# A planner's table of costs and ranks: chained list scatters, gating durations from the trace, a later rank for early gating

## The chip, the core and the metric

The kernel runs on one core of one Trainium2 chip. Five engines work side by side, each through its own instructions in the order in which they were emitted: PE (TensorE, matmuls and transposes into PSUM), DVE (VectorE), ACT (ScalarE), POOL (GpSimd) and SP (SyncE, which here only issues DMAs). They meet through semaphores. The metric is the device time of one execution in microseconds. Times inside a profile are counted from the start of its span.

## What is computed

One transformer block with adaptive layer norm, on x of shape 2 x 2048 x 256 in float32: causal attention with two query heads over one shared key and value head, and then a mixture of eight experts, in which each token uses those experts whose gate lies above a threshold of its own.

```python
sa, ca, ga, sb, cb, gb = six rows of silu(c) @ wmod           # per batch
h = layernorm(x) * (1 + ca) + sa
x = x + ga * attention(h)                                     # causal, rope, 2 heads, D = 256
h = layernorm(x) * (1 + cb) + sb                              # the "hx" of the kernel
gate = softmax(h @ Wg + bg);  thr = sigmoid(h @ Wt + bt) * 0.125
w = max(gate - thr, 0);  w = w / sum(w)                       # 8 experts
x = x + gb * sum_e w_e * (gelu(h @ W1_e + b1_e) @ W2_e + b2_e)
```

## The kernel before

**Two stages.** The 4096 tokens are 32 tiles of 128. In the attention stage every tile is normalised, projected, attended over all earlier tiles of its batch, projected back and normalised again; its rows go to a table in HBM (`feats`), its gate logits to `lg`. Then the experts stage runs hardware loops over lists of tokens: for each expert, items of 256 tokens are gathered from `feats`, turned by a DMA transpose, sent through both weight matrices and added to the output by scatter.

**Groups of tiles.** The tiles come in groups: (0, 4), (1, 4) three times, then two groups of two tiles and four of one, where the first number is the batch and the second the tiles. `q` is the number of tiles before the group, so it is 0, 4, 8, 12, 16 and 20 for the six groups of four. A tile's steps have the rank of its number (`tile_steps`, argument `r`).

**A tile's steps that matter here.** `moments` (L407 to L422) takes mean and variance on DVE (`stats`) and then 1/std on POOL (`rstd`, two small operations, L418 and L419; called `rstda` before attention and `rstdf` after it). `hx` (L667 and L670) is the second normalised row, on DVE; its second operation needs `rstdf`. `halves` (L677, POOL) splits it for the table, `turn_h` (L692, PE) transposes it to `ph`, `logits` (L701, PE) makes the gate logits. Within attention, `score` (L528) makes scores, `keep` (L539, DVE) copies them out and takes their maxima, `top` (L546) joins these to `nmx`, `exp` (L555, ACT) exponentiates, `turn_p` (L601, PE) transposes the probabilities to `ptr`, `pT_out` (L605, ACT) copies them out and `pav` (L611, PE) multiplies by the values.

**Gating of a group** (`gate_steps`, from L716) is six steps: `below` (DVE), `exps` (ACT), `weigh` (DVE; each group's waits for the one before, through `order_w`), `count` (PE, one PSUM bank of the six of the kind "ps", returned by `places`), `spread` (DVE) and `places` (DVE), which writes the place of every token in every expert's list. Then one `scatter` per tile (L807, an indirect DMA that POOL issues) writes the first expert's list, `lists[0]`, in HBM. The lists of the other experts are written later, inside the experts' loops.

**The planner.** No step is emitted at once. `plan.add(engine, cost, do, after, take, give, rank, late)` records it: cost is how long the step holds its engine, `after` names the steps it needs, `take` and `give` count buffers, `late` is time after the cost until its results can be used. `Plan.run` (L59) then plays an imagined clock: whenever an engine is free, the ready step with the lowest rank starts; a result can be used by the next engine 0.12 us later (`LINK`). The order in which steps start there becomes the order of instructions on each engine. Nothing else of the plan reaches the chip: there, engines wait for semaphores, which the framework places by the tiles and tensors that instructions share. Two scatters into `lists[0]` write the same tensor, and so the later one waits on the chip until the earlier one has landed, whether the plan says so or not.

**The end of the stage.** Once the first 24 tiles have been gated, the first 512 entries of the first list are fixed; they are read back (`read_front`, L903) after their scatters, and two items of expert 0 are worked through on PE while the last tiles finish (rank 1000, that is, whenever nothing else is ready). After the last scatter the whole first list is read (L1002), and the next item's rows are gathered, turned and copied to `xT`. Then the experts stage begins.

Of the kernel before, what the change touches and what calls it, by code (L numbers as in the profile page):

```python
# [192 lines left out]
def attention(  # L193
# [16 lines left out]
    def ps_tile(name):  # L210
        return psum.tile([P, 512], F32, tag="ps", name=name)
# [88 lines left out]
    def load_expert(e):  # L300
# [13 lines left out]
        after=[s_sc], rank=first,  # L314
# [24 lines left out]
    for b in range(B):  # L339
# [43 lines left out]
        r = 0.6 + 2 * b  # L383
# [6 lines left out]
    for e in range(RES):  # L390
# [3 lines left out]
                rank=8.0 + 4 * e,  # L394
# [29 lines left out]
    def tile_steps(b, i, r, group, g):  # L424
# [4 lines left out]
        n = (i + 1) * P  # L429
        nch = -(-n // SC)  # L430

        def add(eng, cost, do, after=(), **how):
            return plan.add(eng, cost, do, after=after, rank=r, **how)
# [129 lines left out]
        for h in range(NH):  # L563
            kept = []
            for c in range(nch):
# [4 lines left out]
                    give=["qT"] if (h, c) == (NH - 1, nch - 1) else [],  # L570
# [7 lines left out]
        n_e = {}  # L578
# [16 lines left out]
        def turn_p(c0, m):  # L595
            st["ptr"] = ps_tile(f"ptr{u}_{c0}")
            ptr = st["ptr", c0] = st["ptr"].rearrange("p (c h t) -> p c h t", c=2, h=NH)
            for j in range(m):
                for h in range(NH):
                    s = st["s", h, (c0 + j) * P // SC]  # L600
                    nc.tensor.transpose(ptr[:, j, h, :], s[:, ds((c0 + j) * P % SC, P)], ident)  # L601

        def pT_out(c0, m):
            pT = st["pT", c0] = work([P, 2, NH, P], "pT", f"{u}_{c0}")
            nc.scalar.copy(pT[:, :m], st["ptr", c0][:, :m])  # L605

        def pav(c0, m):
            if c0 == 0:
                st["pav"] = psum_v.tile([P, 512], F32, tag="pav", name=f"pav{u}")
            for j in range(m):  # L610
                nc.tensor.matmul(  # L611
                    st["pav"][:, : NH * P], v[:, c0 + j, :],
                    st["pT", c0][:, j].rearrange("p h t -> p (h t)"),
                    start=(c0 + j == 0), stop=(c0 + j == i),
                )

        n_p = []
        for c0 in range(0, i + 1, 2):
            m = min(2, i + 1 - c0)
            c = c0 * P // SC  # L620
            done = c0 + m == i + 1 or (c0 + m) * P % SC == 0
            n_t = add(
                "PE", 0.155 * 2 * m, lambda c0=c0, m=m: turn_p(c0, m), [n_e[0, c], n_e[1, c]],
                take=["ps"] + (["pav"] if c0 == 0 else []), give=["s", "s"] if done else [],
            )
            n_o = add(
                "ACT", 0.2 + 0.26 * m, lambda c0=c0, m=m: pT_out(c0, m), [n_t], take=["pT"],
                give=["ps"],
            )
            n_p.append(  # L630
                add(
                    "PE", 0.435 * m, lambda c0=c0, m=m: pav(c0, m),
                    [n_o] + n_p[-1:] + [ready_v[b, c0 + j] for j in range(m)], give=["pT"],
                )
            )
# [80 lines left out]
    def gate_steps(b, i0, m, q, group, after):  # L716

        u = f"_{b}_{i0}"
        at = b * NT + i0
        r = q + m - 1.0  # L720
        st = group

        def add(eng, cost, do, after=(), **how):
            return plan.add(eng, cost, do, after=after, rank=r, **how)
# [81 lines left out]
        def scatter(j):  # L806
            nc.gpsimd.indirect_dma_start(  # L807
                out=lists[0],
                out_offset=bass.IndirectOffsetOnAxis(ap=place[:, at + j, 0:1], axis=0),
                in_=entry[:, at + j, 0, :],  # L810
                in_offset=None,
            )

        n = add("DVE", 0.35, below, after)
        n = add("ACT", 0.5, exps, [n])
        n = add("DVE", 1.6, weigh, [n] + order_w)
        order_w[:] = [n]
        n_c = add("PE", 0.3, count, [n], take=["ps"])
        n_w = add("DVE", 1.2, spread, [n])
        n = add("DVE", 1.0, places, [n_c, n_w], give=["ps"])  # L820
        for j in range(m):
            listed.append(plan.add(
                "POOL", 1.27, lambda j=j: scatter(j), after=[n], rank=r + 10.0, late=3.0
            ))
        return n

    order_w, listed, last_exp = [], [], []
    groups = [(0, 4), (1, 4)] * 3 + [(0, 2), (1, 2), (0, 1), (1, 1), (0, 1), (1, 1)]
    begun, q = [0] * B, 0
    for b, m in groups:  # L830
        group, ends = {}, []
        for j in range(m):
            ends.append(tile_steps(b, begun[b] + j, float(q + j), group, j))
        last = gate_steps(b, begun[b], m, q, group, ends)
        begun[b] += m
        q += m
        if q == AHEAD_TILES:
            listed_ahead = list(listed)

            def filled(group=group):  # L840
                pf = ps_tile("pf")
                nc.tensor.matmul(pf[:, :1], ones, group["sum"][:, :1], start=True, stop=True)
                nc.vector.tensor_scalar(flag, pf[:, :1], float(AHEAD * TI), None, ALU.is_ge)

            n_flag = plan.add("PE", 0.2, filled, after=[last], take=["ps"], give=["ps"], rank=q)
# [25 lines left out]
    def low(eng, cost, do, after=(), **how):  # L871
        return plan.add(eng, cost, do, after=after, rank=1000.0, **how)
# [44 lines left out]
    n_w = low("DVE", 0.5, weights_ahead, [n_front, n_flag])  # L917
    before_gelu = list(last_exp)
    for k in range(AHEAD):
# [23 lines left out]
        def first(f0, st=st, k=k):  # L943
            st["ph", f0] = ph = ps_tile(f"pha_{k}_{f0}")
            for f in (f0, f0 + 1):
                for j in range(KD):
                    nc.tensor.matmul(
                        ph[:, ts(f - f0, TI)], weights[0][0][:, j, ts(f, P)], st["xT"][:, j, :],
                        start=(j == 0), stop=(j == KD - 1),
                    )  # L950
# [9 lines left out]
        def second(c, f0, st=st, k=k):  # L960
            if (c, f0) == (0, 0):
                st["py"] = ps_tile(f"pya_{k}")
            for f in range(f0, f0 + NF // 2):
                nc.tensor.matmul(
                    st["py"][:, ts(c, D)], st["g", f // 2 * 2][:, ds(f % 2 * TI + c * P, P)], weights[0][1][:, f, :],
                    start=(f == 0), stop=(f == NF - 1),
                )
# [13 lines left out]
        for f0 in range(0, NF, 2):  # L981
            n = low(
                "PE", 1.74, lambda f0=f0, first=first: first(f0), [n_x, l_first[0]] + before_gelu,
                take=["ps"], give=["s"] if f0 == NF - 2 else [],
            )
# [4 lines left out]
        n = None  # L990
        for c in range(CI):
            for f0 in (0, NF // 2):
                n = low(
                    "PE", 1.74, lambda c=c, f0=f0, second=second: second(c, f0),
                    n_a + ([n] if n is not None else []),
                    take=["ps"] if (c, f0) == (0, 0) else [],
                    give=["s"] * (NF // 2) if (c, f0) == (CI - 1, NF // 2) else [],
                )
# [17 lines left out]
    n = low("DVE", 0.4, behind, [n_s, n_flag])  # L1016
# [405 lines left out]
```

## Time and profile before

| what | us |
|---|---|
| median of three runs | 1696.54 (1695.61 to 1699.3) |
| the profiled execution | 1694.8 |
| its span, first to last instruction | 1693.0 |
| first matmul of the experts' loops | 526.1 |
| last matmul of the attention stage ends at about | 518.8 |
| first and last scatter into the first list start at | 79.9, 504.1 |

The profiled execution is 1.8 us above its span, and 1.7 us below the median of the runs. Everything that the planner orders lies in the first 526 us; the other 1167 us belong to loops whose order is written out by hand. Lines of the timeline have: start, duration, engine, line, operation, output and inputs, count, and in brackets how long the engine stood idle before, and for what.

### The profile page before, as it was taken

Reading aid. Unit: us, or ns where it says so; the run is one execution under the profiler, and the core shown is the slowest. Engines: PE = TensorE matmul, PEld = TensorE weight load, DVE = VectorE, ACT = ScalarE, POOL = GpSimd, SP = SyncE. Lnnn points to the kernel's source line nnn. Section 1 sums busy time; section 2 is a strip of 40 time slices with the busy share of each in tenths; the row PEclk is TensorE's granted clock in tenths of the full one; section 3 lists DMA queues with packets and bytes.
Section 4 is the critical chain, followed back from the end, with each engine's and each line's share of the span. In section 5 each row is a group of like instructions: output and inputs, shape, how many; then the busy total and the mean of one; then the engine's idle time right before and its main releaser. Section 6 shows DMA issues by size and latency. Waiting matters only on the chain.

```text
span 1693.0 us, 26695 instructions
## 1 busy us (share of the span) xinstructions
PE 1627.9 (96%) x7666; PEld 1354.3 (80%) x7666; DVE 677.9 (40%) x2220; ACT 575.1 (34%) x1390; POOL 855.9 (51%) x991
## 2 busy tenths in 40 slices
PE   6898999999998997999999999999999999999997
PEld 3666666677777886888888888888888888888886
DVE  5886666566652322223332222223222232222322
ACT  1544555555551222222222222222322232222222
POOL 2332322111125777765776775676677467744443
PEclk9999999999999998999999999999999999999998
DMA  6310100000013335333434533433533343333333
GB/s 210 102 36 26 38 20 29 22 11 19 14 40 92 59 62 109 56 63 62 103 61 64 109 59 66 106 61 59 106 59 59 65 63 57 64 56 59 65 56 47
DMA packets 166046, 106.36 MB, mean 63 GB/s; under 512 B 111137, under 2 KB 157345, under 8 KB 165857
## 3 DMA queue, kind: packets, MB, share of 16 engines
q0 software_dynamic: 42064, 46.84, 17.3%
q1 hardware_dynamic: 116048, 46.22, 11.8%
q10 hardware_dynamic: 7872, 12.58, 2.3%
q8 instruction: 26, 0.43, 0.1%
q14 instruction: 36, 0.29, 0.1%
HBM read 50.39 MB, written 31.87 MB: 49 GB/s over the span
## 4 chain that ended last, share of the span: by engine, by line
PE 60%; DMA 3%; POOL 2%; issue 2%; POOLq 0%; DVE 0%; SPq 0%; DVEq 0%
PE h L1142 30%; PE y L1133 30%; DMA xp<-xr 2%; POOL out L1285 1%; DMA xr<-feats,at 1%; POOL list L1275 0%; DMA out<-yo,who 0%; POOL xr L1254 0%; POOLq L1035 0%; POOL out L1317 0%; POOL at L1296 0%; POOLq L1083 0%; POOLq L1296 0%; DVE yo L1232 0%; DVE xT L896 0%
## 5 line engine op out<-in xcount | busy, mean ns | idle before, releaser
L1142 PE MATMUL h<-xT,w 128*128 128x256 f32 (+1 forms) x2752 | 659.8, 373 | 16.3 <-DVE xT L1196 9.0
L1133 PE MATMUL y<-w,g 128*128 128x256 f32 x2640 | 654.2, 379 | 0.0
L1168 ACT ACTIVATE g<-h,b_sb 128x256 f32<-128x256 f32 (+1 forms) x688 | 319.6, 465 | 847.5 <-PE h L1142 844.8
L1142 PEld LDWEIGHTS h<-xT,w 128*128 128x128 f32 x2752 | 515.6, 192 | 85.4 <-DVE xT L1196 10.5
L1133 PEld LDWEIGHTS y<-w,g 128*128 128x128 f32 x2640 | 499.2, 190 | 65.2
L1285 POOL DMA_INDIRECT out<-yo,who x173 | 283.0, 1636 | 212.8 <-DVE yo L1232 160.6
L1196 DVE COPY xT<-xp 128x512 uint16<-128x512 uint16 x172 | 68.4, 439 | 613.9 <-PE h L1142 581.2
L1275 POOL DMA_INDIRECT list<-new,to x228 | 235.4, 1032 | 99.3 <-POOL new L1270 46.7
L1254 POOL DMA_INDIRECT xr<-feats,at x172 | 173.7, 1010 | 100.9 <-POOL at L1296 70.2
L611 PE MATMUL pav<-pT,v 128*128 128x256 f32 x544 | 144.8, 389 | 0.5 <-ACT pT L605 0.5
L528 PE MATMUL psc<-kT,qT 128*128 128x512 f32 (+3 forms) x320 | 144.2, 536 | 0.6 <-ACT qT L517 0.2
L539 DVE TENSOR_SCALAR_CACHE_REDUCE s<-psc 128x512 f32<-128x512 f32 (+3 forms) x160 | 95.8, 605 | 78.1 <-PE psc L528 59.2
L555 ACT ACTIVATE s<-s,nmx 128x512 f32<-128x512 f32 (+3 forms) x160 | 103.8, 651 | 53.7 <-DVE nmx L546 53.4
L611 PEld LDWEIGHTS pav<-pT,v 128*128 128x128 f32 x544 | 95.9, 192 | 26.3 <-issue 16.4
L1220 DVE TENSOR_TENSOR yb<-y,b_bc 128x256 f32<-128x256 f32 x165 | 62.7, 420 | 132.4 <-PE y L1133 132.4
L605 ACT COPY pT<-ptr 128x512 f32<-128x512 f32 (+1 forms) x144 | 76.8, 563 | 50.9 <-PE ptr L601 28.9
L418 POOL TENSOR_SCALAR rstdf<-mvf 128x1 f32<-128x1 f32 x32 | 8.7, 270 | 166.7 <-DVE mvf L414 70.5
L807 POOL DMA_INDIRECT list<-entry,place x32 | 33.8, 1056 | 101.3 <-DVE place L804 75.1
L601 PEld LDWEIGHTS ptr<-ident,s 128*128 128x128 f32 x544 | 65.4, 143 | 21.3 <-ACT s L555 8.7
L601 PE MATMUL ptr<-ident,s 128*128 128x128 f32 x544 | 76.6, 277 | 4.5 <-ACT s L555 4.4
L1211 DVE SCALAR_TENSOR_TENSOR gate<-gb_bc,mcur,part 128x256 f32<-128x256 f32 x172 | 75.8, 482 | 3.0
L528 PEld LDWEIGHTS psc<-kT,qT 128*128 128x128 f32 x320 | 56.9, 191 | 15.3 <-issue 6.2
(157 smaller groups left out, 1076.1 us busy)
## 6 DMA issues: line engine op xcount, KB each, us to landing
w<-in_w ACTq DMA_DIRECT2D x12, 1024.0 KB, 8.0
x<-in_x SPq DMA_DIRECT2D x32, 128.0 KB, 2.1
out<-x SPq DMA_DIRECT2D x32, 128.0 KB, 1.7
w<-in_w SPq DMA_DIRECT2D x4, 1024.0 KB, 9.1
feats<-hp SPq DMA_DIRECT2D x32, 128.0 KB, 1.7
list<-new,to POOLq DMA_INDIRECT x228
out<-yo,who POOLq DMA_INDIRECT x173, 3.9
xr<-feats,at POOLq DMA_INDIRECT x172, 2.8
```

The lines of the kernel that those rows point to most:

```text
L528: nc.tensor.matmul(ps[:, :w], st["qT"][:, h, :], kT[:, ds(c * SC, w)], start=True, stop=not last)
L539: nc.vector.tensor_scalar(s[:, :w], st["sc", h, c][:, :w], 1.0, None, ALU.mult, ALU.max, accum_out=st["mx", h][:, c : c + 1],)
L555: nc.scalar.activation(s[:, :w], s[:, :w], AF.Exp, bias=st["nmx", h], accum_out=st["den"][:, h, c : c + 1],)
L601: nc.tensor.transpose(ptr[:, j, h, :], s[:, ds((c0 + j) * P % SC, P)], ident)
L605: nc.scalar.copy(pT[:, :m], st["ptr", c0][:, :m])
L611: nc.tensor.matmul(st["pav"][:, : NH * P], v[:, c0 + j, :], st["pT", c0][:, j].rearrange("p h t -> p (h t)"), start=(c0 + j == 0), stop=(c ...
L1133: last = pe.matmul(ys[c], gs[f % 4][:, ts(c, P)], weights[e][1][:, f, :], start=(f == 0), stop=(f == NF - 1),)
L1142: last = pe.matmul(hs[f % 4][:, :w], weights[e][0][:, k, ts(f, P)], xT[:, k, :w], start=(k == 0), stop=(k == KD - 1),)
L1168: act.activation(gs[f % 4][:, :w], hs[f % 4][:, :w], AF.Gelu_apprx_tanh, bias=b1_sb[:, at : at + 1],).then_inc(sem["act"], 1)
L1254: pool.indirect_dma_start(out=xr[:, ts(c, 2 * D)], out_offset=None, in_=feats, in_offset=bass.IndirectOffsetOnAxis(ap=at[:, c : c + 1], ax ...
L1275: pool.indirect_dma_start(out=lists[e], out_offset=bass.IndirectOffsetOnAxis(ap=to[:, j : j + 1], axis=0), in_=new[:, j, :], in_offset=Non ...
L1285: pool.indirect_dma_start(out=rows, out_offset=bass.IndirectOffsetOnAxis(ap=who[:, c : c + 1], axis=0), in_=yo[:, c, :], in_offset=None, b ...
```

## The change

Three kinds of edit, all in numbers that the planner reads; no instruction's work is altered.

- Scatters into the first list: each now names the scatter before it as one that it needs; the cost goes from 1.27 to 1.1 and the lateness from 3.0 to 1.5.
- Durations: `below` 0.35 to 0.4, `weigh` 1.6 to 1.4 + 0.2 per tile of the group (2.2 for four tiles, 1.8 for two, 1.6 for one), `spread` 1.2 to 1.4, `places` 1.0 to 1.2; a transpose in `turn_p` 0.155 to 0.12.
- Rank of gating: for groups of four tiles it is raised by 8 - 2 * (q // 8): by 8 for q = 0 and 4, by 6 for 8 and 12, by 4 for 16 and 20. Ranks of gating are then 11, 15, 17, 21, 23 and 27 where they were 3, 7, 11, 15, 19 and 23. The scatters' rank stays 10 above it.

```diff
-                "PE", 0.155 * 2 * m, lambda c0=c0, m=m: turn_p(c0, m), [n_e[0, c], n_e[1, c]],
+                "PE", 0.12 * 2 * m, lambda c0=c0, m=m: turn_p(c0, m), [n_e[0, c], n_e[1, c]],
...
-        r = q + m - 1.0
+
+        r = q + m - 1.0 + (8.0 - 2.0 * (q // 8) if m == 4 else 0.0)
...
-        n = add("DVE", 0.35, below, after)
+        n = add("DVE", 0.4, below, after)
         n = add("ACT", 0.5, exps, [n])
-        n = add("DVE", 1.6, weigh, [n] + order_w)
+        n = add("DVE", 1.4 + 0.2 * m, weigh, [n] + order_w)
         order_w[:] = [n]
         n_c = add("PE", 0.3, count, [n], take=["ps"])
-        n_w = add("DVE", 1.2, spread, [n])
-        n = add("DVE", 1.0, places, [n_c, n_w], give=["ps"])
+        n_w = add("DVE", 1.4, spread, [n])
+        n = add("DVE", 1.2, places, [n_c, n_w], give=["ps"])
+
         for j in range(m):
             listed.append(plan.add(
-                "POOL", 1.27, lambda j=j: scatter(j), after=[n], rank=r + 10.0, late=3.0
+                "POOL", 1.1, lambda j=j: scatter(j), after=[n] + listed[-1:], rank=r + 10.0,
+                late=1.5,
             ))
```

## Prediction

> **What bounds the kernel now.** I read the page first, then the stretches of time, then who waits for whom on TensorE, then single holes.
>
> ```profile
> span 1693.0 us, 26695 instructions
> ...
> PE 1627.9 (96%) x7666; PEld 1354.3 (80%) x7666; DVE 677.9 (40%) x2220; ACT 575.1 (34%) x1390; POOL 855.9 (51%) x991
> ...
> PEclk9999999999999998999999999999999999999998
> ```
>
> PE (the matmuls) is busy for 96% of the span. So time can only come from its holes, from its clock or from its work, and this change alters no work: it edits costs and ranks with which a planner orders instructions. Where are the holes? The stretches (busy time of PE, PEld, DVE, ACT, POOL, then clock and DMA) say: in the attention stage, early.
>
> ```profile
> 50.00:100.00 50.00, 44.21 (x205) 29.75 (x203) 41.94 (x162) 22.26 (x70) 19.87 (x38) 0.93 0.16 48
> 100.00:150.00 50.00, 45.47 (x223) 32.92 (x222) 34.87 (x131) 24.68 (x71) 13.12 (x24) 0.93 0.09 28
> 350.00:400.00 50.00, 50.00 (x233) 34.61 (x232) 30.49 (x113) 27.36 (x78) 9.24 (x14) 1.00 0.05 17
> ...
> 700.00:900.00 200.00, 200.00 (x943) 176.71 (x942) 60.51 (x164) 55.65 (x120) 135.31 (x145) 1.00 0.39 70
> ```
>
> From 526 us on the experts run in loops that the planner doesn't order. Attention has PE idle of 5.8 us in 50-100, 4.5 in 100-150, 2.8 in 150-200, none in 350-450; with 5.1 in 25-50, 1.6, 2.3 and 1.2 in the three stretches from 200 to 350, and 2.6 in 450-500, it is 25.9 us between 25 and 500. PE's waits there:
>
> ```profile
> PE ph L692 <- DVE nmx L546: 5.4, 2, 4.4
> PE ptr L601 <- ACT s L555: 4.4, 3, 2.1
> PE ph L692 <- DVE hx L670: 4.3, 5, 1.9
> PE ph L692 <- DVE rd L588: 3.5, 2, 2.2
> ```
>
> The transpose ph of the second normalised rows hx accounts for 13.2 us, in nine holes. Its releaser is labelled differently, but the operand is always hx. The largest hole, followed backwards on PE, VectorE (DVE) and GpSimd (POOL), in three timelines:
>
> ```profile
> 132.71 0.66 PE L692 MATMUL ph<-ident,hx 128*128 128x128 f32 x2 [4.39 <-DVE nmx L546]
> ```
> ```profile
> 125.98 0.18 DVE L414 BATCH_NORM_AGGREGATE mvf<-stf 128x2 f32<-128x6 f32 x1
> ...
> 132.07 0.49 DVE L670 SCALAR_TENSOR_TENSOR hx<-hx,rstdf,mod_bc 128x256 f32<-128x256 f32 x1 [4.46 <-POOL rstdf L419]
> ```
> ```profile
> 122.23 1.10 POOL L807 DMA_INDIRECT list<-entry,place  x1 [1.29 <-DVE place L804]
> 124.74 0.97 POOL L807 DMA_INDIRECT list<-entry,place  x1 [1.41 <-DMA list<-entry,place]
> 127.12 0.96 POOL L807 DMA_INDIRECT list<-entry,place  x1 [1.41 <-DMA list<-entry,place]
> 130.16 0.96 POOL L807 DMA_INDIRECT list<-entry,place  x1 [2.08 <-DMA list<-entry,place]
> 131.14 0.25 POOL L418 TENSOR_SCALAR rstdf<-mvf 128x1 f32<-128x1 f32 x1
> ```
>
> The moments mvf were there at 126.16. The small POOL pair that makes 1/std from them (0.8 us) ran at 131.14, because the third and fourth scatter of the first list stood before it in POOL's queue, each waiting until the one before had landed. DVE stood 4.46 us, with the next tile's score maxima behind hx; PE 4.39. The plan had booked those four scatters as 1.27 us each, back to back, and so believed POOL free after 5.1 us; here the fourth started 7.9 us after the first.
>
> **What the Trainium skill says.** "DMA: Bandwidth & Descriptors", section "Two DMAs through the same engine are not ordered": ordering comes from the issuing engine waiting on the first DMA's semaphore. The trace agrees: 20 of the 32 scatters are not first in their group, and POOL idled 26.2 us before them (1.31 each) for the scatter ahead. The same page, "Anatomy of one DMA — SWDGE (gpsimd) path", puts a fixed cost of about 2.0 us on such a DMA, mostly the receipt of the write; measured here 2.1 to 2.8, median 2.2, to landing. "TensorE: Matmul & The Clock Gate", section "What's actually happening": after an idle window of about 3.4 us the clock falls to half until PE has been busy about as long. Here the clock drops behind the two stretches with the most idle time and not behind a hole of 2.2 us (last line):
>
> ```profile
> 80.00:90.00 10.00, 6.45 (x20) 4.61 (x20) 6.77 (x25) 3.97 (x12) 6.04 (x7) 0.66 0.09 27
> 126.00:140.00 14.00, 9.61 (x41) 6.59 (x41) 7.16 (x27) 6.64 (x18) 4.39 (x9) 0.76 0.10 30
> 170.00:180.00 10.00, 7.67 (x39) 5.21 (x38) 7.26 (x28) 6.45 (x20) 4.82 (x6) 1.00 0.13 40
> ```
>
> **The change part by part.**
>
> *Scatters that know of each other* (chain, cost 1.1, late 1.5). Planned distance becomes 1.1 + 1.5 + 0.12 (the plan's link) = 2.72 us, with POOL open for 1.6 us between. Measured distance: 2.4 to 2.5 as a rule, up to 3.0. So a 1/std that becomes ready between scatters is emitted between them. Five groups show a held 1/std (mvf ready, started): 81.21 and 84.00; 126.16 and 131.14; 170.90 and 174.93; 222.35 and 225.40; 286.31 and 289.81: delays 2.8, 5.0, 4.0, 3.1, 3.5. The PE holes behind them: 1.26, 4.39, 2.22, 1.62, 1.88, together 11.4 us. Each delay exceeds its hole; even if the 1/std still waits out one scatter of 1.1 us, only 4.39 - (4.98 - 1.1) = 0.5 us stays. Gain: 11 us. A scatter pushed behind a 1/std loses nothing that anyone awaits: the list is first read at 471.44, and all scatters but the last few land 40 us or more earlier. Every scatter's DMA and POOL's queue with it move with the chain; SP's queue is not passed.
>
> *Gating ranked later, with longer costs.* One four-tile gating is some 20 small DVE operations of about 0.18 us: below 0.4, weigh 2.0, spread 1.25, places 1.35, about 5 us. No operation is added. Group 0 stands ahead of maxima at 73-80, while DVE is 84% busy; PE holes there are 0.80 (74.59), 1.02 (81.39) and 1.27 (82.99), and group 5's count has 0.88 at 344. Later rank should let the maxima pass, but DVE has no less to do in 50-100. Bounds: 0 and 4.0; I take half, 2.0. From about 150 us DVE is three quarters busy or less, so the rank decides little there. The cover of a moved gating is DVE's idle time; if that is gone, up to 5 us per group reappear somewhere on PE.
>
> *Transposes at 0.12 for 0.155.* A set of four takes PE 0.43 us from its start to the start of the next work, 0.108 each, so 0.12 is nearer. The plan's PE gets 544 x 0.035 = 19 us shorter; the chip's does not. Direct worth nothing; it reshuffles everything after the first tiles.
>
> *Clock.* Busy time times missing clock in 5-us stretches: 80-90: 2.03 x 0.23 + 4.42 x 0.46 = 2.5; 130-140: 2.29 x 0.45 + 5.00 x 0.24 = 2.2; together 4.7. It goes if those holes go: 3.5 taken.
>
> *What the new order opens.* No row prices this. The holes that are not explained above are 25.9 - 11.4 - 4.0 = 10.5 us; that is what such a plan leaves by itself. I charge 40% more of it, 4 us; bounds 0 and 10.
>
> Sum: 11 + 2 + 3.5 - 4 = 12.5 us. Does it reach the end? PE's last work on the items done ahead ends at 518.8, DVE closes them and copies xT until 521.0, and the experts' first matmul starts at 526.1: all of it follows PE. The other chain (last scatter 504.13, list read 506.60, gather 512.23, transpose 516.41, xT) starts at the last tile's gating and comes forward with it. Afterwards the experts keep PE full. So it is one for one. The profiled execution took 1694.8 (span 1693.0), so 1682.3; the median is 1696.54, 1.7 above it, so **1684**.
>
> **The rivals.**
>
> *All of it, nothing opened*: 11.4 + 4.0 + 4.7 = 20 us, 1677. For it: each hole has one named cause. Against: DVE's 84%, and a reshuffle that is never free. 0.10.
>
> *The holes only move*: plan and chip drift apart by more than the 0.2 to 0.3 us between planned and measured distance, 1/stds again stand behind scatters, and what is gained at five places is lost at others. Between 5 faster and 3 slower, about 1695. For it: drift exists (POOL waits 75.1 us for place, up to 10.5 at once, though mostly with nothing behind it). 0.16.
>
> *Slower: PSUM.* The gating's count takes one of six banks and returns it only when places has read it. That was 2.4 us in group 0 (76.58 to 78.97). Ranked eight tiles later, count may run in a hole of PE while places waits behind busier DVE work, and the scores have five banks. A bank's share is a sixth, so one us held costs PE at most some 0.17. To cancel 16.5 us of gains takes 99 us of holding, 25 us in each of the four first groups; beyond that it is slower. At 30 us each it is 120 x 0.17 = 20 us lost, 3.5 net, 1700. Against: PE's waits for a freed bank are hardly seen (psc on s: 0.2 us), and 25 us is more than two tiles' time there (the hp copies of ten tiles run from 36 to 133 us). 0.12.
>
> **How the numbers follow.** My forecast has 0.62 and its own bounds: gains 11 to 18, new holes up to 7, so 1678 to 1692. The range 1677 to 1695 adds the full gain and the better half of "only move". The measurement can tell about 0.2% (3.4 us) from no change. Faster by more: 0.62 + 0.10 + 0.04 = 0.76; within: 0.12, from "only move"; slower: 0.12.
>
> **What would show it.** Right: between scatters 1/std pairs on POOL; DVE's wait for rstdf (16.7 us) below 6; PE's waits for ph below 4; clock 1.00 from 80 to 140; the experts' first matmul near 514. Wrong: the ph holes stay at 10 us or more, or new ones on psc, pr or ptr take their room; or the bank from count to places stands for 25 us. If ph's holes go and the clock does not come back, the clock step alone was wrong.

## The result and the profile after

The changed kernel takes 1677.0 us, median of five runs (1675.83 to 1677.69), against 1695.98 for the kernel before in the same set. The ratio is 0.9883, 95% interval 0.987 to 0.9897, so 17 to 22 us less. The kernel before itself took 1695 to 1697 us in most sets of runs and 1714 us in two of them, so every kernel below is compared, as a ratio, with the kernel before run beside it. The profiled execution has a span of 1675.2 us where it had 1693.0. The numbers of lines in the changed kernel's views lie one to three higher than before.

The page first, its span and each engine's busy time:

```profile
span 1675.2 us, 26699 instructions
...
PE 1622.3 (97%) x7666; PEld 1352.3 (81%) x7666; DVE 677.0 (40%) x2220; ACT 576.4 (34%) x1390; POOL 855.0 (51%) x991
```

PE runs the same 7666 instructions. Of the 17.8 us that left the span, 12.2 are idle time of PE (65.1 to 52.9) and 5.6 are busy time (1627.9 to 1622.3). Where, the stretches say (PE, PEld, DVE, ACT, POOL, clock, DMA); the last two lines are the stretches in which the prediction saw the clock drop before:

```profile
50.00:100.00 50.00, 47.23 (x249) 34.38 (x248) 45.28 (x176) 26.91 (x83) 15.46 (x32) 1.00 0.17 56
100.00:150.00 50.00, 48.51 (x225) 33.81 (x225) 38.91 (x147) 25.27 (x73) 20.30 (x36) 0.97 0.10 30
...
80.00:90.00 10.00, 9.33 (x47) 6.37 (x46) 8.83 (x42) 5.76 (x17) 0.94 (x2) 1.00 0.10 30
126.00:140.00 14.00, 14.00 (x65) 9.60 (x63) 9.45 (x31) 7.01 (x18) 7.36 (x13) 0.99 0.10 29
```

PE has 249 matmuls between 50 and 100 us where it had 205, and DVE, too, is busier (45.28 us for 41.94): the same work is done sooner. PE's idle time from 25 to 500 us fell from 25.9 to 13.6. What is left of its waits from 20 to 500 us (total, times, longest), and the wait of hx for its 1/std from 20 to 510:

```profile
PE pt L453 <- DVE xn L444: 3.1, 3, 2.4
PE ptr L601 <- ACT s L555: 2.7, 3, 2.1
PE ph L692 <- DVE s L539: 1.4, 2, 0.7
...
PE ph L692 <- DVE hx L670: 0.3, 1, 0.3
PE ph L692 <- ACT pT L605: 0.3, 1, 0.3
```
```profile
DVE hx L670 <- POOL rstdf L419: 2.5, 4, 0.8
```

All of ph's waits come to 2.0 us (13.2 before), hx's for `rstdf` to 2.5 (16.7). POOL's timeline shows why, in the scatters of the second group, the ones that held a 1/std for 5 us before:

```profile
125.49 1.09 POOL L808 DMA_INDIRECT list<-entry,place  x1 [5.32 <-DVE place L805]
126.61 0.25 POOL L418 TENSOR_SCALAR rstda<-mva 128x1 f32<-128x1 f32 x1
126.94 0.57 POOL L419 TENSOR_TENSOR rstda<-rstda,neg_half 128x1 f32<-128x1 f32 x1
127.98 1.07 POOL L808 DMA_INDIRECT list<-entry,place  x1 [0.47 <-DMA list<-entry,place]
129.66 0.29 POOL L418 TENSOR_SCALAR rstda<-mva 128x1 f32<-128x1 f32 x1 [0.60 <-DVE mva L414]
130.03 0.57 POOL L419 TENSOR_TENSOR rstda<-rstda,neg_half 128x1 f32<-128x1 f32 x1
130.79 1.08 POOL L808 DMA_INDIRECT list<-entry,place  x1 [0.19 <-issue]
134.56 0.22 POOL L418 TENSOR_SCALAR rstdf<-mvf 128x1 f32<-128x1 f32 x1 [2.69 <-DVE nmx L546]
134.86 0.57 POOL L419 TENSOR_TENSOR rstdf<-rstdf,neg_half 128x1 f32<-128x1 f32 x1
135.62 1.07 POOL L808 DMA_INDIRECT list<-entry,place  x1 [0.19 <-issue]
```

Every pause between two scatters has a 1/std in it, and the fourth scatter stands behind a 1/std that was not yet ready instead of ahead of it. The experts start where the attention stage lets them (durations in ns, least, median and greatest, then first and last start in us):

```profile
L1145 PE MATMUL h<-xT,w x2752: 272/379/796, 506.9 to 1661.0; 128*128 128x256 f32 x182, 128*128 128x128 f32 x15
```

First matmul at 506.9 (526.1), 19.2 us sooner; from there to the end of the span it takes 1.4 us longer than before.

### The profile page after: what moved, and what is told of

The parts are those of the page before. It is cut to its first block, busy times and chain, and to the rows that moved or that the text cites. A ratio compares the mean times of both kernels' runs of the same rounds, so it can differ in the third digit from the quotient of the medians.

```text
span 1675.2 us, 26699 instructions
## 1 busy us (share of the span) xinstructions
PE 1622.3 (97%) x7666; PEld 1352.3 (81%) x7666; DVE 677.0 (40%) x2220; ACT 576.4 (34%) x1390; POOL 855.0 (51%) x991
## 3 DMA queue, kind: packets, MB, share of 16 engines
q0 software_dynamic: 42064, 46.84, 17.8%
## 4 chain that ended last, share of the span: by engine, by line
PE 61%; DMA 3%; issue 3%; POOL 3%; POOLq 1%; DVE 0%; SPq 0%; DVEq 0%
PE h L1145 31%; PE y L1136 30%; POOL out L1288 2%; DMA xp<-xr 1%; DMA xr<-feats,at 1%; POOL list L1278 0%; POOL xr L1257 0%; DMA out<-yo,who 0%; POOLq L1038 0%; POOL out L1320 0%; POOL at L1299 0%; POOLq L1086 0%; POOLq L1299 0%; DVE yo L1235 0%; POOL to L1270 0%
## 5 line engine op out<-in xcount | busy, mean ns | idle before, releaser
L1145 PEld LDWEIGHTS h<-xT,w 128*128 128x128 f32 x2752 | 514.7, 191 | 86.6 <-DVE xT L1199 10.5
```

Of the source, the lines that this page charges most:

```text
L1145: last = pe.matmul(hs[f % 4][:, :w], weights[e][0][:, k, ts(f, P)], xT[:, k, :w], start=(k == 0), stop=(k == KD - 1),)
```

## The experiments

The change has four parts, which are tried alone and left out: **S** (the scatters), **R** (the rank of gating), **D** (gating's durations) and **T** (0.12 for a transpose of `turn_p`). The rivals at this stage: S takes the holes away and the rest is small, as the forecast had it; R does it; or every kernel of this family is a draw, since any new number reorders the whole stage. To tell a draw from a cause, some kernels also set `LINK` to 0.13 for 0.12, a number that corrects nothing named above and reorders everything. All numbers are in this table. "Start" is the experts' first matmul; "gating" is the time from the start of the first DVE operation of `below` to the start of the last of `places`, summed over the six groups of four; "held" is DVE's waits for `rstdf` and `rstda` from 20 to 510 us; "idle" is PE's waits from 20 to 500 us. Start, gating, held and idle come from one profile of each kernel and are in us.

| kernel | ratio | 95% interval | start | gating | held | idle |
|---|---|---|---|---|---|---|
| before | 1 | | 526.1 | 38.4 | 19.3 | 25.5 |
| the change, S R D T | 0.9883 | 0.987 to 0.9897 | 506.9 | 137.1 | 3.0 | 12.8 |
| only_chain: S | 0.9977 | 0.9964 to 0.999 | 525.2 | 39.7 | 8.6 | 21.5 |
| only_rank: R | 0.9932 | 0.9907 to 0.9958 | 521.2 | 124.5 | 11.3 | 18.3 |
| only_dur: D | 0.9995 | 0.9979 to 1.001 | 525.8 | 39.5 | 13.2 | 21.2 |
| only_ptr: T | 0.9938 | 0.9916 to 0.996 | 514.5 | 38.6 | 11.5 | 18.9 |
| no_chain: R D T | 0.9971 | 0.9961 to 0.9982 | 521.8 | 130.0 | 19.3 | 21.1 |
| no_rank: S D T | 0.9976 | 0.9966 to 0.9986 | 523.1 | 40.3 | 7.7 | 22.4 |
| no_dur: S R T | 0.9903 | 0.9886 to 0.9919 | 509.9 | 105.2 | 4.2 | 16.1 |
| no_ptr: S R D | 0.9899 | 0.9882 to 0.9916 | 508.7 | 116.2 | 5.4 | 11.9 |
| rank_chain: S R | 0.9907 | 0.9888 to 0.9926 | 510.4 | 118.5 | 5.6 | 13.2 |
| ptr_190: 0.19 in place of 0.155 | 1.0028 | 1.0016 to 1.004 | 531.6 | 39.2 | 21.0 | 26.4 |
| all_true: S R D T, three more transposes | 0.9914 | 0.9898 to 0.9931 | 509.2 | 95.5 | 6.6 | 11.5 |
| before_link13 | 0.9981 | 0.9973 to 0.9988 | 523.1 | 38.6 | 11.1 | 22.8 |
| only_chain_l13: S | 0.9932 | 0.9915 to 0.9949 | 517.9 | 38.1 | 6.7 | 16.9 |
| only_rank_l13: R | 0.998 | 0.9968 to 0.9992 | 523.6 | 98.1 | 10.8 | 19.0 |
| only_ptr_l13: T | 0.9989 | 0.9977 to 1.0001 | 524.2 | 42.6 | 10.7 | 23.1 |
| rank_chain_l13: S R | 0.992 | 0.9899 to 0.994 | 507.5 | 114.0 | 9.8 | 12.3 |
| after_link13: S R D T | 0.9893 | 0.9861 to 0.9925 | 508.6 | 111.7 | 6.7 | 13.5 |

Each ratio is against the kernel before, link 0.12, run beside it. The kernels whose neighbour took 1714 us are the four parts alone, only_ptr_l13 and after_link13. In their profiles the stretch from the experts' first matmul to the end of the span is 1180.6 to 1195.4 us long, in all others 1166.5 to 1169.6: the extra time lies in the experts' stage, behind the start and outside the columns on the right.

**Each part alone.**

```diff
-                "POOL", 1.27, lambda j=j: scatter(j), after=[n], rank=r + 10.0, late=3.0
+                "POOL", 1.1, lambda j=j: scatter(j), after=[n] + listed[-1:], rank=r + 10.0,
+                late=1.5,
```


> Only the scatters' part of the change (each names the one before it, cost 1.1, late 1.5); durations, transposes and ranks as before. Hold theory (the gain is 1/std pairs that no longer stand behind waiting scatters): 11 to 15 us faster than before, 1681 to 1685; DVE's wait of hx for rstdf falls from 16.7 us below 6, PE's waits for ph from 13.2 below 4. Rank theory (the gain is gating that leaves DVE in the tight stretch from 50 to 130 us): at most 5 us faster, clock still low at 80 to 90. Transposes theory (the gain is the better cost of the transposes and the order it makes): within 3 us of before.


```diff
-        r = q + m - 1.0
+        r = q + m - 1.0 + (8.0 - 2.0 * (q // 8) if m == 4 else 0.0)
```


> Only the later rank of gating and its scatters. Hold theory: 0 to 4 us faster, the groups whose scatters still stand ahead of an rstdf keep their holes. Rank theory: 10 us faster or more, PE's idle time from 50 to 150 us falls from 10.3 below 5. Transposes theory: within 3 us of before.


```diff
-        n = add("DVE", 0.35, below, after)
+        n = add("DVE", 0.4, below, after)
...
-        n = add("DVE", 1.6, weigh, [n] + order_w)
+        n = add("DVE", 1.4 + 0.2 * m, weigh, [n] + order_w)
...
-        n_w = add("DVE", 1.2, spread, [n])
-        n = add("DVE", 1.0, places, [n_c, n_w], give=["ps"])
+        n_w = add("DVE", 1.4, spread, [n])
+        n = add("DVE", 1.2, places, [n_c, n_w], give=["ps"])
```


> Only the longer planned durations of below, weigh, spread and places. All theories: within 3 us of before. If it alone brings 5 us or more, the planner's clock was late on DVE and that was the cause of the held 1/stds.


```diff
-                "PE", 0.155 * 2 * m, lambda c0=c0, m=m: turn_p(c0, m), [n_e[0, c], n_e[1, c]],
+                "PE", 0.12 * 2 * m, lambda c0=c0, m=m: turn_p(c0, m), [n_e[0, c], n_e[1, c]],
```


> Only the planned cost of a transpose, 0.12 for 0.155. Hold and rank theories: nothing by itself, within 4 us of before either way, and the size of that is what a mere reshuffle costs. Transposes theory: 8 us faster or more.

S, which the forecast priced at 11 us, brought 0.0023 x 1696 = 3.9 us. Its own effect is there, DVE's wait for `rstdf` falls from 16.7 to 5.1 us, but PE's idle time falls by 4.0 only. R alone brought 11.5 us with more than half of the holding left in place (11.3 of 19.3 us), T alone 10.5 us although it names no step of the chain at all. D alone did not change the time, although PE idles 4.3 us less in its profile, as much as with S. So the split of the forecast is wrong, and alone the parts do not show why.

**One part left out of the change.** Diffs against the changed kernel:

```diff
-                "POOL", 1.1, lambda j=j: scatter(j), after=[n] + listed[-1:], rank=r + 10.0,
-                late=1.5,
+                "POOL", 1.27, lambda j=j: scatter(j), after=[n], rank=r + 10.0, late=3.0
```


> The whole change but for the scatters' part: no naming of the scatter before, cost 1.27, late 3.0. Hold theory: holds come back, hx waits 8 us or more for rstdf, and the experts start at 513 us or later. Transposes theory: they start within 4 us of 506.9.


```diff
-        r = q + m - 1.0 + (8.0 - 2.0 * (q // 8) if m == 4 else 0.0)
+        r = q + m - 1.0
```


> The whole change but for the rank. Pair theory: the gating stands in one block on DVE again (5 to 8 us from ngm to place), and 5 us or more of the 20 are lost: 5 to 14 us faster than before. Transposes theory: 17 us faster or more.


```diff
-        n = add("DVE", 0.4, below, after)
+        n = add("DVE", 0.35, below, after)
...
-        n = add("DVE", 1.4 + 0.2 * m, weigh, [n] + order_w)
+        n = add("DVE", 1.6, weigh, [n] + order_w)
...
-        n_w = add("DVE", 1.4, spread, [n])
-        n = add("DVE", 1.2, places, [n_c, n_w], give=["ps"])
+        n_w = add("DVE", 1.2, spread, [n])
+        n = add("DVE", 1.0, places, [n_c, n_w], give=["ps"])
```


> The whole change but for the durations of gating. All theories: within 3 us of the changed kernel, that is 16 to 22 us faster than before. More than 5 us lost would mean that the durations matter once the scatters are chained.


```diff
-                "PE", 0.12 * 2 * m, lambda c0=c0, m=m: turn_p(c0, m), [n_e[0, c], n_e[1, c]],
+                "PE", 0.155 * 2 * m, lambda c0=c0, m=m: turn_p(c0, m), [n_e[0, c], n_e[1, c]],
```


> The whole change but for the transposes' cost, which is 0.155 again. Transposes theory (PE work booked longer than it is lets the plan put other work in front of what PE will soon need): the experts start at 514 us or later, 7 us or more after the changed kernel's 506.9. Hold theory: within 3 us of 506.9, since no 1/std is held. Sum of parts taken alone (0.9 + 4.9 + 0.3): 520.

Without S, 4.9 of 19.8 us are left; without R, 4.1; without D or T, 16.5 and 17.1. With D and T in place, S and R are needed, both. The trace of the kernel without R shows, at one second row, what is left when S is there. DVE, POOL and PE around one second row:

```profile
77.30 1.00 DVE L652 SCALAR_TENSOR_TENSOR x<-po,rd,x 128x256 f32<-128x256 f32 x2 [0.29 <-PE po L645]
78.22 0.17 DVE L772 TENSOR_SCALAR ge<-ge 128x32 f32<-128x32 f32 x1
...
79.83 0.18 DVE L414 BATCH_NORM_AGGREGATE mvf<-stf 128x2 f32<-128x6 f32 x1
79.93 0.16 DVE L792 TENSOR_TENSOR off<-on,back 128x32 f32<-128x32 bf16 x1
...
81.09 0.19 DVE L804 CUSTOM_DVE_ANT_0 place<-place,col 128x64 uint16<-128x64 uint16 x1
81.20 0.48 DVE L667 SCALAR_TENSOR_TENSOR hx<-x,mvf,mod_bc 128x256 f32<-128x256 f32 x1
81.78 0.48 DVE L670 SCALAR_TENSOR_TENSOR hx<-hx,rstdf,mod_bc 128x256 f32<-128x256 f32 x1
```
```profile
80.41 0.57 POOL L419 TENSOR_TENSOR rstdf<-rstdf,neg_half 128x1 f32<-128x1 f32 x1
81.59 1.25 POOL L807 DMA_INDIRECT list<-entry,place  x1 [0.61 <-DVE place L804]
```
```profile
82.42 0.41 PE L692 MATMUL ph<-ident,hx 128*128 128x128 f32 x2 [3.61 <-DVE hx L670]
```

POOL had the 1/std at 80.98, before its first scatter. It is DVE that is late: twelve small operations of gating stand between `x` and `hx`, from 78.22 to 79.37 and from 79.93 to 81.20, together 2.4 us, against PE's hole of 3.61. In the changed kernel the same `x` is made at 77.34, gating stands still between 76 and 84 us, DVE makes score maxima in that room, and PE's hole before that `ph` (81.45) is 0.30. The row itself gains only part of this: its `hx` is done at 81.39 in place of 82.26, and the rest of the hole is filled by scores and transposes that PE has there ahead of `ph`. Gating of the first group spreads over 23.4 us (6.1 before).

And without S, with R, POOL's timeline, and PE behind it:

```profile
99.53 1.25 POOL L807 DMA_INDIRECT list<-entry,place  x1 [1.46 <-DVE place L804]
102.22 0.99 POOL L807 DMA_INDIRECT list<-entry,place  x1 [1.44 <-DMA list<-entry,place]
103.24 0.25 POOL L418 TENSOR_SCALAR rstda<-mva 128x1 f32<-128x1 f32 x1
...
108.76 1.02 POOL L807 DMA_INDIRECT list<-entry,place  x1 [1.64 <-DMA list<-entry,place]
109.81 0.25 POOL L418 TENSOR_SCALAR rstdf<-mvf 128x1 f32<-128x1 f32 x1
```
```profile
107.81 0.44 PE L453 MATMUL pt<-ident,xn 128*128 128x128 f32 x2 [1.27 <-DVE xn L444]
...
111.37 0.66 PE L692 MATMUL ph<-ident,hx 128*128 128x128 f32 x2 [2.05 <-DVE rd L588]
```

The scatters, which DVE now releases later, hold the 1/stds of the next tiles as before: 12.2 us of DVE's waits for `rstda`, 7.1 for `rstdf`. So there are two places that hold a row, DVE with gating and POOL with the scatters, and each trace shows one at work where the other was removed. In idle time of PE, the waits for `ph` make 6.6 of the 9.6 us that the kernel without R has more than the changed one, and 4.4 of 8.3 without S. That PE's queue of other work bridges one of the two as a rule, and not both, is an inference from these rows and is not shown.

**S and R together, and more of what D and T do.** The first kernel has the diffs of only_chain and only_rank. The second goes the wrong way with T, the third adds the three other kinds of transposes, by the same start-to-start time, to the changed kernel.

> Only two parts of the change, the scatters' and the rank; durations and transposes as before. Pair theory (the gating's block of operations on DVE and the scatters on POOL delay the same hx one after the other, and PE's queue can cover one of them but not both): 15 to 19 us faster than before, nearly all of the change. Transposes theory: at most 9 us faster.


```diff
-                "PE", 0.155 * 2 * m, lambda c0=c0, m=m: turn_p(c0, m), [n_e[0, c], n_e[1, c]],
+                "PE", 0.19 * 2 * m, lambda c0=c0, m=m: turn_p(c0, m), [n_e[0, c], n_e[1, c]],
```


> The kernel before with a transpose booked at 0.19 in place of 0.155, further from the 0.108 that it takes. Transposes theory: slower, the experts start at 530 us or later and PE waits more than 28 us in all between 20 and 500. Reshuffle theory (any other order has a fair chance to be better than this one): between 515 and 527.


```diff
-        n_t = add("PE", 0.32, turn, [n_n], take=["ps"], give=["xn"])
+        n_t = add("PE", 0.24, turn, [n_n], take=["ps"], give=["xn"])
...
-        n_t = add("PE", 0.48, turn_rot, [n_r], take=["ps"], give=["big"])
+        n_t = add("PE", 0.36, turn_rot, [n_r], take=["ps"], give=["big"])
...
-            n_t = add("PE", 0.32, turn_h, [n_h], take=["ps"])
+            n_t = add("PE", 0.24, turn_h, [n_h], take=["ps"])
```


> The changed kernel with the other transposes booked at 0.12 each as well: turn and turn_h 0.24 for 0.32, turn_rot 0.36 for 0.48. If a truer table helps by itself, 2 to 6 us faster than the changed kernel (0.9850 to 0.9875 of before); if the rest is a matter of which order comes out, within 4 us either way.

The pair brought 15.8 us. That is also the sum of S and R alone (3.9 + 11.5), so with D and T out the two look like separate gains; only with D and T in (4.1 without R and 4.9 without S, against 19.8) does each need the other. A transpose booked too long cost 4.7 us. Truer costs for the other transposes lost 5.3 us of the change (0.9914 against 0.9883, with intervals just apart), so a truer plan is not a better one by itself.

**The same parts in another order.** Each of these is its kernel above with

```diff
-        LINK = 0.12
+        LINK = 0.13
```


> The kernel before with the plan's link between engines at 0.13 in place of 0.12 and nothing else: another order by a cause that has nothing to do with gating. If the parts' times are the luck of an order, this moves by 5 us or more, most likely to faster; by the pair theory it keeps both delays and stays within 4 us of before.

> Link 0.13 and the scatters' part alone. Pair theory: 2 to 6 us faster than before, as with 0.12. Luck: anything between 3 slower and 15 faster.

> Link 0.13 and the later rank alone, on a second chip. Pair theory: 3 to 12 us faster than before, and less than with both parts by 4 us or more. Luck: no order between this and the others.

> Link 0.13 with the scatters' part and the rank. Pair theory: 13 to 19 us faster than before, the fastest of the four. Luck: not faster than the better of the two single parts.

> Before with the turn_p cost of 0.12 alone and the link at 0.13. If the 10 us of the turn_p cost alone were a fortunate order, they shrink to what the link alone brings or less: ratio 0.996 or more, first matmul at 520 or later. If the truer cost itself brings them, they stay: ratio 0.995 or less, first matmul at 517 or earlier, holds of the 1/std at 12 or less.

> The whole change with the planner's link at 0.13 for 0.12, which reshuffles the order and corrects no disturbance. Theory (two delays in series, both taken away together): the order that comes out does not matter much, so ratio 0.983 to 0.993, the experts' first matmul at 503 to 513, idle time of TensorE from 20 to 500 us at 16 or less. Rival (the change drew a lucky order): the reshuffle loses most of it, ratio 0.995 or more, first matmul after 518.

The link by itself brought 3.2 us. In the new order S alone brings 11.5 us, where 2 to 6 were expected, and R alone 3.4 against the kernel before, the reverse of the old order; T's 10.5 us shrink to 1.9, less than the link alone. So the size of a single part is mostly the order it happens to meet. What does not move is the combination: the seven kernels with S and R have ratios from 0.9883 to 0.992 (13.6 to 19.8 us), the eleven that lack one or both from 0.9932 to 1.0028; only the intervals of the nearest kernels of the two sorts overlap. PE idles 11.5 to 16.1 us in the seven and 16.9 to 26.4 in the eleven. In the new order the pair is only 2.0 us ahead of S alone, which is within the intervals. The whole change keeps 18.1 of its 19.8 us in the other order. D and T on top of the pair are worth 4.0 us in the one order and 4.5 in the other; twice the same sign, within the intervals.

The kernel before also ran once more with nothing changed:

> The kernel before, unchanged, for a profile on the chip of this set. The first expert matmul starts at 526 us within 1, as in its first profile, and DVE waits 16 to 17 us with hx for rstdf; if the start differs by 3 us or more, starts of the experts can't be compared between chips.

It took 1700.38 us, with its start at 530.3 instead of 526.1. PE's idle time is the same (25.7 us for 25.5), and so are DVE's waits for `rstdf` (16.2 for 16.7) and PE's for `ph` (13.1 for 13.2). The difference is the clock: busy time times missing clock, summed in stretches of 1 us up to the start, is 12.2 us here and 6.7 in the first profile. At 74 us, for example, the first profile (upper lines) and the second have the same hole and another clock after it:

```profile
74.59 0.55 PE L512 MATMUL pr<-ident,t 128*128 128x128 f32 x3 [0.80 <-DVE before L752]
74.00:78.00 4.00, 3.41 (x18) 2.60 (x19) 3.55 (x21) 1.49 (x5) 0.00 (x0) 1.00 0.00 0
```
```profile
73.91 0.70 PE L512 MATMUL pr<-ident,t 128*128 128x128 f32 x3 [0.79 <-DVE before L752]
74.00:78.00 4.00, 4.00 (x14) 2.80 (x15) 3.05 (x17) 0.92 (x3) 0.00 (x0) 0.57 0.00 0
```

So a start of one profile is good to some 4 us, while this repeat gave PE's idle time back within 0.2. The same sum says why the start of D alone did not move: its profile loses 13.0 us to the clock.

## Why the prediction was off in size

The direction held, and so did the signs named in advance. The time was 7 us below the number given and at the lower edge of its range of 1677 to 1695 us (0.9883 of the 1696.54 us that the forecast started from is 1676.7). By its own steps:

- **Holds behind scatters, and gating ranked later, 11 + 2 = 13 us: right in the sum, wrong in the split.** With S and R together PE idles 12.3 us less. There are 2.5 us of waits for `rstdf` (below 6), 2.0 for `ph` (below 4), and 1/std pairs between scatters. But S alone brings 3.9 or, against its own order, 0.0049 x 1696 = 8.3 us, and R, given 2 with bounds of 0 and 4, brings 11.5 or 0.2. The reading that failed here was to take the wait that ended last as the price of the whole hole. DVE's gating ahead of the same rows was seen in the trace and priced only where it showed as a hole of its own.
- **What the new order opens, minus 4 (bounds 0 and 10): the step that failed.** With the 13 us taken, 25.9 - 13 + 4 = 16.9 us of idle time were to remain between 25 and 500; the profile has 13.6. Only 0.7 of the 4 were given back. The charge was made because DVE is 84% busy from 50 to 100 us; it is 91% busy after, and PE idles less.
- **Clock, plus 3.5: the other term that was mis-sized.** By the same sum (busy time times missing clock in 5-us stretches, from 40 to 460 us) the loss fell from 4.7 to 2.3, so 2.4 came back; in 1-us stretches up to the experts it is 6.7 and 5.1, only 1.6. The clock is full at 80 to 90 and 130 to 140, but low at 123 to 126 and, newly, at 457 to 460. The term took it for granted that the clock follows the holes; in the kernel before, two executions with nearly the same holes differ by 5.5 us in this loss (12.2 and 6.7), more than the whole term.
- **PE's busy time apart from the clock, put at nothing because the change alters no work.** Up to the experts, busy time fell by 6.7 us (482.3 to 475.6), of which the clock explains 1.6 to 2.4. 1.1 is in `pg`, sixteen matmuls between 19 and 26 us (4.9 to 3.8), and that is luck: with the same work ahead of it `pg` takes 3.8 us with S alone and 5.6 with R alone. The rest is spread over rows in parts below 1.5 us, and its cause stays open.
- **Transposes at 0.12, direct worth nothing.** Nothing shows a direct worth: only_ptr_l13 is at 0.9989. In the changed kernel T and D together may be worth 4 us as part of a plan nearer to the chip, or as another draw of the order: all_true, nearer still, is 5.3 us behind it.
- **One for one to the end: right.** Idle and busy time give 3.3 and 3.2 us more than forecast, and the start at 506.9 lies 6.7 before the 513.6 that the forecast implies; 1.4 of it is lost again in the experts' stage.
- **The rivals.** "All of it, nothing opened" named 1677 and came closest, with 0.10; but of the 4.7 us of clock in its list only 1.6 to 2.4 came back, so the agreement is in part luck. "The holes only move" is what S without R does where D and T are in: no_rank has as little waiting for `rstdf` as the change (2.5 us) and 22.4 us of idle time. The PSUM rival did not come about: from `count` to `places` the bank stood for 4 to 5 us in the first four groups (119.56 to 124.36 in the second), not 25, although gating stretched up to 45.6 us, since the plan let `count` go late too.

What stays open is how much of the 19.8 us is a good order, and how much of it is a clock that happened to hold. Two orders say 18 to 20; two are few.

## What to carry to other kernels

The trace shows for a late operand the wait that ended last, and its length need not be what removing it will bring (here 11 us were booked, and 3.9 or 8.3 came): follow the operand back to its source and price everything that stands ahead of it on every engine it passes. In a stage ordered by a planner, a part tried alone mostly measures the order it falls into (here 10.5 us or 1.9 for the same edit): repeat it under a change of order that corrects nothing before believing its size. Compare idle time and clock apart: one repeat gave the same idle time within 0.2 us, while the loss to the clock moved by 5.5. Ranking a block of small operations below the work that feeds the bottleneck is worth trying even on a nearly full engine: DVE was 84% busy from 50 to 100 us and is 91% busy now, while PE idles less.

## What was not expected of the hardware

The clock fell behind smaller holes than expected. "TensorE: Matmul & The Clock Gate", section "What's actually happening", speaks of an idle window of about 3.4 us. In the changed kernel the only holes above 0.15 us between 107 and 169 us are of 0.62 and 0.46 us, at 120 and 121, and yet:

```profile
120.00:130.00 10.00, 9.15 (x41) 6.96 (x42) 7.67 (x30) 4.27 (x11) 3.44 (x6) 0.83 0.09 28
...
123.00:126.00 3.00, 3.00 (x13) 2.53 (x12) 2.79 (x13) 2.07 (x5) 0.51 (x1) 0.50 0.00 0
```

The mean of 0.83 is about 3.4 us at half clock among full clock (0.99 in the microsecond before 123, 0.81 in the one after 126). Before, a hole of 2.22 us between 170 and 180 left the clock at 1.00. A hole of 2.12 us before the same transposes left it at 1.00 in the kernel before (at 476.9) and was followed by half clock in the changed one (at 457.1). And the two executions of the kernel before differ in clock behind the same hole of 0.8 us. Read as the length of one hole, the page's window does not fit, and the trace decides: the length of a single hole is not what sets the clock in this stage, and the order of the instructions alone is not either. What does was not tried. One thing to try: from 119.6 us to the fall at 123, and from 69 to the fall at 74 in the second profile of the kernel before, PE ran nothing but transposes and matmuls of at most 32 columns.

A transpose's record is not its price for PE: records of `ptr` are 280 ns long on average in the changed kernel, and the next work starts 0.43 us after four of them, 0.108 us each.
